# A mixed order of tiles in layer 1 of a graph attention kernel

## The chip, the cores and the metric

The kernel runs on one core of a Trainium2 chip. The core has five engines with a queue of instructions each: TensorE (PE in the profile; its weight loads are shown apart as PEld), VectorE (DVE), ScalarE (ACT), GpSimd (POOL) and SyncE (SP), and 16 DMA engines that all queues share. Instructions of one engine run in order; engines wait for each other by semaphores. The metric is the device time of one execution in microseconds (us).

## The reference

Two layers of graph attention (GAT) over 10,000 nodes with 768 numbers each and 170,000 edges (80,000 random pairs in both directions, and a self-loop for each node), sorted by destination. Layer 1 has 4 heads of 256, layer 2 one head of 768. Cut to what matters:

```python
def gat_conv(x, edge_index, W, a_src, a_dst, bias, heads, out_ch, concat):
    ei = _add_self_loops(edge_index, n)
    src, dst = (ei[0], ei[1])
    xl = (x @ W).reshape(n, heads, out_ch)
    alpha_src = einsum('nhc,hc->nh', xl, a_src)
    alpha_dst = einsum('nhc,hc->nh', xl, a_dst)
    e = leaky_relu(alpha_src[src] + alpha_dst[dst], 0.2)
    m = segment_max(e, dst)
    e = exp(e - m[dst])
    alpha = e / (segment_sum(e, dst)[dst] + 1e-16)
    out = segment_sum(xl[src] * alpha[:, :, None], dst)
    return out + bias
...
h = gat_conv(x, edge_index, W1, a_src1, a_dst1, b1, HEADS, HID, True)
h1 = relu(layer_norm(h, g1, be1)) + (x @ Wr1 + br1)
h = gat_conv(h1, edge_index, W2, a_src2, a_dst2, b2, 1, OUT_DIM, False)
h = layer_norm(h, g2, be2) + (h1 @ Wr2 + br2)
return _layernorm(x + h)
```

## The kernel before

**Preparation** (up to about 760 us). A table is computed, `table1`: for each node a row of 1,033 numbers (4,132 bytes) with its 1,024 projected features, its attention terms and its rank. Beside it the nodes are counted and ranked by how many edges end in them, most edges first. The 10,000 nodes make 79 tiles of 128 nodes in rank order, so the nodes of a tile have about the same number of edges. A tile t gets a fixed number of slots, `SLOTS[t]`, from a bound on the number of edges at that rank: 41 for tile 0, 27 for tile 1, then 26, 25, 24 and so on down to 7 for tile 78, 1,371 in all. A slot is one row for each of the 128 nodes: the row of one neighbour. The word "rows" of the change means these slots. `slots` (128 x 1,371 integers) lists the neighbours to gather, tile after tile in the order of `TURNS`; `FIRST[t]` is the first column of a tile.

**Layer 1** (`ordered_layer1`) goes through the tiles in the order of `TURNS`; a position in that order is what its loop counts as `t`. Before, `TURNS` takes every second tile from the smallest to the largest and the others back again: 7, 10, 11, 12, 12, 13, ... 22, 22, 23, 24, 26, 41, 27, 25, 24, 23, 22, 22, ... 12, 12, 11, 11, 9 rows. For each slot POOL issues one indirect DMA (`gather`, L472) that brings 128 rows of `table1` into one of the 31 places of `ring` (`RING1`); `ring.fetch`, called once a slot, issues the gather for a place as soon as the row that lay there has been used, so up to 31 rows are on their way or waiting. For positions 1 and 2 a limit of their own, `upto`, holds fetches back.

What is done for a tile at position t:

- `weights_of` makes the attention weights: POOL adds the terms (`summed_logits`, L939 to L944), DVE and ACT take the leaky maximum, the exponent and the sum (`exponents`, L956). It is begun during the last rows of the tile before (`soon`, three or four rows before its end).
- Tiles of 22 rows or more (`PARTED`) do this in groups: two groups, the last of 8 rows, or three groups of 17, 12 and 12 for the 41 (`cuts_of`). A later group is rescaled into the sum of the earlier ones (L1204), and its first one to three rows are summed by PE and copied by ACT (L1014).
- The first rows of a tile, none up to five (`on_pe`: 0 for 11 rows, 1 for 12 and 13, 2 for 14 and 15, 3 for 16 and 17, 4 for 18 and 19, 5 from 20 on), are scaled by ACT in place (L562, four scalings a row, one for each head) and summed by PE in PSUM with an identity matrix (L933). The other rows are added by DVE: either scaled by ACT first and added in one instruction (L569), or scaled and added by DVE (L573).
- Meanwhile the tile before is finished: its statistics (L584, two instructions a tile, on DVE), its normalisation and residual (L598, L600, L1078) make `h`; PE transposes `h` (L896), computes the residual product of the present tile `x @ Wr1` (L179) and multiplies `h` by W2 (L1150, `to_layer2`); ACT copies the outcome (L1042), and SP stores it as a part of `table2` (L1044) and stores `hT` (L1142) for layer 2.
- In a tile without groups, PE also transposes the x of the next tile ahead of time (`turn`); behind a tile with groups this is done at the start of the next tile.

**Layer 2** (`ordered_layer2`) goes over the tiles again in an order of its own, `turns`, which is made by sorting the positions of layer 1 by size and taking large and small ones by turns; it gathers rows of `table2` by rank and writes the result.

The lines that set the order before the change:

```python
    TURNS = list(range(NT - 1, -1, -2))
    TURNS += sorted(set(range(NT)) - set(TURNS))
    FIRST, TOTAL = [0] * NT, 0
    for t in TURNS:
        FIRST[t], TOTAL = TOTAL, TOTAL + SLOTS[t]
```

Of the kernel before, what the change touches and what calls it, by code (L numbers as in the profile page):

```python
# [57 lines left out]
WHOLE = 4  # L58
PARTED = 22
FEW = 11  # L60


def chunk_counts(n_edges):
# [23 lines left out]
def gnn_kernel(ctx, tc, x, x_cols, src, dst, src_col, dst_col, W1, a_src1, a_dst1, b1, g1, be1, Wr1, br1,  # L87
# [9 lines left out]
    NT = -(-N // P)  # L97
# [3 lines left out]
    CAPS = slot_counts(N, n_edges)  # L101
    SLOTS = CAPS

    TURNS = list(range(NT - 1, -1, -2))
    TURNS += sorted(set(range(NT)) - set(TURNS))
    FIRST, TOTAL = [0] * NT, 0
    for t in TURNS:
        FIRST[t], TOTAL = TOTAL, TOTAL + SLOTS[t]
# [446 lines left out]
    def doubled(e, t):  # L555
        nc.vector.tensor_scalar(e[:, 0], e[:, 0], loops[:, TURNS[t]:TURNS[t] + 1], None, op0=OP.mult)

# [276 lines left out]

    SLOTS, FIRST = [SLOTS[t] for t in TURNS], [FIRST[t] for t in TURNS]
    SLOTS1, FIRST1 = SLOTS, FIRST
    turns = sorted(range(NT), key=lambda t: SLOTS[t] + 2 * (t >= NT - 2))
    first, left, final = turns[:3], turns[3:-3] + turns[-1:], turns[-3:-1]
    mean, mixed = sum(SLOTS[t] for t in left) / len(left), []
    while left:  # L840
        few = sum(SLOTS[t] for t in mixed) <= mean * len(mixed)
# [27 lines left out]
    def nodes(t):  # L869
        return order[:, TURNS[t]:TURNS[t] + 1]  # L870

    def ordered_layer1(mem):
        nc.scalar.add_instruction(mybir.InstLoadActFuncSet(name=nc.get_next_instruction_name(), act_func_set_id=6, engine=nc.scalar.engine))
        with tc.tile_pool(name="b1", bufs=1) as pool, tc.tile_pool(name="small1", bufs=2) as small, \
# [42 lines left out]
            def on_pe(t):  # L917


                return min(max(SLOTS[t] // 2 - 5, int(SLOTS[t] > FEW)), ON_PE1)  # L920

# [25 lines left out]
            def exponents(e, top=None):  # L947

                n = e.shape[1]
                leaky(e, e)  # L950
                new = small.tile([P, H1], F32, name="new")
                nc.vector.reduce_max(new, e.rearrange("p k h -> p h k"), axis=AX.X)
                if top is not None:
                    nc.vector.tensor_max(new, new, top)
                nc.vector.tensor_tensor(e, e, new[:, None, :].to_broadcast([P, n, H1]), op=OP.subtract)
                nc.scalar.activation(e, e, AF.Exp)  # L956
                return new

            def weights_of(t):
# [11 lines left out]
                top = exponents(e)  # L971
                nc.scalar.activation(e[:, 0], e[:, 0], AF.Copy, scale=loops[:, TURNS[t]:TURNS[t] + 1])
                yield {0: (e, None)}
# [722 lines left out]
```

## Time and profile before

| | |
|---|---|
| median of 3 runs | 5296.87 us (5289.57 to 5301.86) |
| the profiled execution, its own time | 5288.65 us |
| span of the profiled execution | 5286.9 us |
| mean granted clock of TensorE | 0.946 |
| HBM read and written | 1426.26 MB and 177.29 MB |
| DMA of the software queue (gathers) | 1283.72 MB |

The page gives, for the slowest core of one execution, the busy time of each engine and its share of the span. Below stand 40 equal slices of the span (132 us each), where a digit is the busy share in tenths; the row PEclk is the clock that TensorE was granted, in tenths of full speed. Groups of instructions are named by line, engine, operation and the tiles written and read (`out<-in`), with the number of instructions, the busy time and the mean duration. Idle time of an engine is put down to what released it (`<-`). A view of stretches gives the busy times, the granted clock and the DMA figures for any part of the span.

### The profile page before, as it was taken

How to read it: one execution, taken by the hardware profiler on the slowest of the kernel's cores; microseconds unless marked ns; L12 is line 12 of the kernel's file. 1: busy time of each engine (PE TensorE's matmuls, PEld its weight loads, DVE VectorE, ACT ScalarE, POOL GpSimd, SP SyncE). 2: the span in 40 equal slices, each digit the busy share in tenths (PEclk: the TensorE clock that was granted, in tenths of full speed). 3: DMA queues.
4: the chain of work that ended last, by engine and by line, in shares of the span. 5: the costliest groups of instructions: out<-in, count | busy, mean ns of one | idle time of the engine just before them, and what ended most of it. 6: DMA issues, size and time to landing. Idle time of an engine off the chain costs nothing. (4 is left out here: it accounts for less than half of the span.)

```text
span 5286.9 us, 58012 instructions
## 1 busy us (share of the span) xinstructions
PE 4759.0 (90%) x14100; PEld 2659.8 (50%) x14100; DVE 4343.1 (82%) x7341; ACT 2986.1 (56%) x8450; POOL 3429.6 (65%) x3722
## 2 busy tenths in 40 slices
PE   9999988999999978899999997888888888888886
PEld 4444444555544434444555554555555555555554
DVE  7887877999989988889999985877777776777776
ACT  5744446888889988898888762232222222222222
POOL 6877756666677766677666626666666666666664
PEclk9999999999999998999999998898899898888898
DMA  4423459999999989999999959988898888888885
GB/s 153 131 98 127 113 176 337 350 358 369 381 379 393 376 298 339 342 367 377 382 367 360 351 213 313 325 320 316 314 321 315 311 313 310 312 305 300 306 312 191
DMA packets 433439, 1588.37 MB, mean 300 GB/s; under 512 B 77207, under 2 KB 82135, under 8 KB 433094
## 3 DMA queue, kind: packets, MB, share of 16 engines
q0 software_dynamic: 321040, 1283.72, 67.7%
q1 hardware_dynamic: 99490, 269.38, 14.1%
q10 hardware_dynamic: 12564, 31.47, 1.9%
q8 instruction: 119, 1.95, 0.2%
q14 instruction: 226, 1.85, 0.1%
HBM read 1426.26 MB, written 177.29 MB: 303 GB/s over the span
## 5 line engine op out<-in xcount | busy, mean ns | idle before, releaser
L472 POOL DMA_INDIRECT ring<-table,slots x2663 | 2633.5, 989 | 1496.1 <-issue 564.8
L562 ACT ACTIVATE ring<-ring,e 128x256 f32<-128x256 f32 x4208 | 1714.4, 502 | 62.9 <-DVE e L978 36.6
L573 DVE SCALAR_TENSOR_TENSOR acc<-ring,e,acc 128x256 f32<-128x256 f32 (+1 forms) x2540 | 1581.3, 623 | 106.4 <-PE acc L933 21.5
L569 DVE TENSOR_TENSOR acc<-acc,ring 128x1024 f32<-128x1024 f32 x782 | 962.9, 1231 | 77.9 <-ACT ring L562 17.6
L1342 PE MATMUL big<-wr,w 128*128 128x512 f32 (+1 forms) x2464 | 870.0, 499 | 129.2 <-issue 127.7
L1288 PE MATMUL big<-ring,diagonals 128*128 128x256 f32 x2742 | 723.6, 419 | 187.7 <-issue 172.6
L1150 PE MATMUL half<-w,hT 128*128 128x512 f32 (+1 forms) x2528 | 842.5, 486 | 3.6 <-issue 3.5
L179 PE MATMUL big<-wr,xT 128*128 128x512 f32 x1896 | 836.6, 598 | 0.3 <-ACT xT L897 0.3
L1288 PEld LDWEIGHTS big<-ring,diagonals 128*128 128x128 f32 x2742 | 581.5, 213 | 324.5 <-issue 226.1
L1287 ACT ACTIVATE diagonals<-ident,e 128x128 f32<-128x128 f32 x1371 | 420.6, 388 | 533.6 <-PE big L1288 227.0
L1342 PEld LDWEIGHTS big<-wr,w 128*128 128x128 f32 x2464 | 478.1, 195 | 484.7 <-issue 455.2
L1150 PEld LDWEIGHTS half<-w,hT 128*128 128x128 f32 x2528 | 472.6, 189 | 346.4 <-issue 310.6
L179 PEld LDWEIGHTS big<-wr,xT 128*128 128x128 f32 x1896 | 358.5, 193 | 422.3 <-issue 421.6
L933 PE MATMUL acc<-ring,ident 128*128 128x512 f32 x1080 | 495.9, 609 | 58.5 <-ACT ring L562 51.4
L588 ACT ACTIVATE sd<-mv,eps 128x1 f32<-128x1 f32 x237 | 69.3, 292 | 688.5 <-issue 362.0
L933 PEld LDWEIGHTS acc<-ring,ident 128*128 128x128 f32 x1080 | 205.8, 194 | 307.4 <-issue 188.5
L694 ACT ACTIVATE scr<-scr 128x256 f32<-128x256 f32 x624 | 250.5, 403 | 160.5 <-DVE scr L687 152.5
L634 PE MATMUL one<-wr,mixed 128*128 128x512 f32 x702 | 307.6, 592 | 0.0
L699 POOL TENSOR_TENSOR row<-row,none 128x1024 f32<-128x1024 f32 x69 | 168.1, 2437 | 115.2 <-DVE scr L687 45.0
L634 PE MATMUL one<-w,xT 128*128 128x512 f32 x492 | 226.8, 597 | 7.9 <-DMA w<-in_W_dram 5.6
L584 DVE BATCH_NORM_STATS2 st<-big 128x6 f32<-128x256 f32 x79 | 33.4, 422 | 234.4 <-remote 125.6
L634 PEld LDWEIGHTS one<-wr,mixed 128*128 128x128 f32 x702 | 133.4, 190 | 167.9 <-issue 166.9
(239 smaller groups left out, 4328.1 us busy)
## 6 DMA issues: line engine op xcount, KB each, us to landing
ring<-table,slots POOLq DMA_INDIRECT x2663
h_d<-hT SPq DMA_DIRECT2D x79, 512.0 KB
table<-row SPq DMA_DIRECT2D x78, 516.0 KB
w<-h_d SPq DMA_DIRECT2D x77, 512.0 KB
table<-row SPq DMA_DIRECT2D x79, 385.0 KB
ring<-table SPq DMA_DIRECT2D x79, 385.0 KB
x_d<-xt SPq DMA_DIRECT2D x77, 384.0 KB
w<-x_d SPq DMA_DIRECT2D x77, 384.0 KB
```

The lines of the kernel that those rows point to most:

```text
L179: nc.tensor.matmul(p[:, c:e], aT[:, j, :], w[:, j, c:e], start=(j == 0), stop=(j == k - 1))
L472: nc.gpsimd.indirect_dma_start(out=to, out_offset=None, in_=table, in_offset=bass.IndirectOffsetOnAxis(ap=index, axis=0), **more)
L562: nc.scalar.activation(row[:, s], row[:, s], AF.Copy, scale=e[:, h:h + 1])
L569: nc.vector.tensor_add(acc[:, :c], acc[:, :c], row[:, :c])
L573: nc.vector.scalar_tensor_tensor(acc[:, s], row[:, s], e[:, h:h + 1], (acc if first is None else first)[:, s], op0=OP.mult, op1=OP.add)
L634: nc.tensor.matmul(p, aT[:, j, :], w[:, j, :], start=(start and j == 0), stop=(j == k - 1), skip_group_check=True)
L694: nc.scalar.activation(m[:, s], m[:, s], AF.Copy, accum_out=row[:, C1 + i * H1 + h:C1 + i * H1 + h + 1])
L933: nc.tensor.matmul(acc[:, c:c + BANK], ident, ring.slot(q + k)[:, c:c + BANK], start=(k == 0), stop=(k == m - 1))
L1150: nc.tensor.matmul(q, hT[:, j, :], w2[:, j, c:c + q.shape[1]], start=(j == 0), stop=(j == K1 - 1))
L1287: nc.scalar.activation(diagonals[:, (k - lo) % G, :], ident, AF.Copy, scale=e[:, k - lo, :])
L1288: nc.tensor.matmul(to, diagonals[:, (k - lo) % G, :], ring.slot(at + k)[:, ON_PE2:C2], start=False, stop=(k == n - 1), skip_group_check=True)
L1342: nc.tensor.matmul(r[:, c:d], hT[:, j, :], wr2[:, j, c:d], start=False, stop=(j == K1 - 1 and d < C2), skip_group_check=True)
```

## The change

Only `TURNS` is made in another way. Seven tiles are set aside for the two ends (`ENDS`): the smallest four of every second one (7, 10, 11, 12 rows) begin and 11, 11, 9 end. The 72 others are picked one by one: from the largest while the mean of those picked is not above the mean of all tiles, otherwise from the smallest. The list is then turned round, so that the largest tile comes last in it.

```diff
+ENDS = 7
...
-    TURNS = list(range(NT - 1, -1, -2))
-    TURNS += sorted(set(range(NT)) - set(TURNS))
+    TURNS, few, left = [], [NT - 1 - t for t in range(min(ENDS, NT))], list(range(NT - len(range(min(ENDS, NT)))))
+    while left:
+        more = sum(SLOTS[t] for t in TURNS) <= sum(SLOTS) * len(TURNS) / NT
+        TURNS.append(left.pop(0 if more else -1))
+    TURNS = few[::2] + TURNS[::-1] + few[1::2][::-1]
```

The rows of the tiles in order, after:

```
7 10 11 12 22 21 21 21 21 20 20 20 20 20 20 19 19 19 19 19 19 18 18 18 18 18 18 18 18 17 17 17 17 17 17 17 16
22 16 16 16 22 16 16 16 16 22 15 15 23 15 15 23 15 15 15 24 14 14 24 14 14 25 14 14 13 26 13 13 27 13 13 12 12 12 41 11 11 9
```

## The prediction, made before the change was run

> **What bounds the kernel now.** I read the page's totals and slices first.
>
> ```profile
> span 5286.9 us, 58012 instructions
> PE 4759.0 (90%) x14100; PEld 2659.8 (50%) x14100; DVE 4343.1 (82%) x7341; ACT 2986.1 (56%) x8450; POOL 3429.6 (65%) x3722
> PE   9999988999999978899999997888888888888886
> PEclk9999999999999998999999998898899898888898
> DMA  4423459999999989999999959988898888888885
> ```
>
> PE is 90% busy over the whole span, but the change touches layer 1 alone, so the question is what paces that stage. In the slices it runs from about 760 to 3150 us, with PE and DMA near full except for a dip around 1850 to 2250, where the 22- to 41-row tiles stand together. Where a tile ends I read from the first of its two statistics on DVE (L584, two a tile); I cut the trace at those. First four longer stretches of layer 1, then its middle tile by tile (columns: stretch and length, busy time of PE, weight loads, DVE, ACT, POOL with their counts, granted clock, DMA share, GB/s).
>
> ```profile
> L584 DVE BATCH_NORM_STATS2 st<-acc x38: 679/689/699, 1699.2 to 2402.1; 128x6 f32<-128x512 f32 x38
> ...
> 906.10:1248.90 342.80, 339.07 (x1037) 179.02 (x1036) 315.91 (x457) 280.15 (x714) 220.39 (x274) 1.00 0.97 354
> 1480.50:1732.63 252.13, 245.52 (x714) 124.23 (x713) 224.41 (x313) 232.73 (x593) 180.46 (x216) 1.00 1.01 387
> 1877.80:2157.40 279.60, 231.31 (x607) 112.08 (x606) 235.36 (x404) 230.51 (x580) 186.47 (x245) 0.91 0.89 319
> 2157.40:2236.20 78.80, 68.68 (x183) 33.59 (x183) 65.54 (x114) 63.51 (x162) 51.96 (x67) 0.93 0.94 337
> ...
> 1699.19:1732.63 33.44, 31.40 (x91) 15.54 (x90) 28.48 (x38) 30.95 (x79) 22.81 (x28) 1.00 1.01 387
> 1732.63:1767.90 35.27, 33.75 (x93) 16.51 (x92) 32.51 (x56) 32.56 (x84) 25.78 (x36) 1.00 0.99 364
> 1767.90:1802.50 34.60, 33.22 (x95) 16.39 (x95) 32.48 (x56) 31.96 (x82) 25.45 (x35) 1.00 1.01 385
> 1802.50:1839.20 36.70, 33.45 (x95) 16.42 (x95) 34.50 (x61) 32.21 (x82) 26.80 (x37) 1.00 0.99 377
> 1839.20:1877.80 38.60, 36.01 (x101) 17.53 (x101) 34.57 (x61) 34.64 (x88) 27.97 (x35) 1.00 0.97 366
> 1877.80:1922.50 44.70, 37.87 (x101) 18.27 (x100) 35.89 (x62) 36.14 (x92) 26.81 (x37) 0.96 0.89 322
> 1922.50:1990.30 67.80, 42.31 (x110) 19.84 (x109) 56.77 (x97) 55.62 (x141) 48.11 (x64) 0.84 0.73 252
> 1990.30:2037.30 47.00, 43.49 (x110) 20.69 (x109) 37.90 (x66) 37.98 (x96) 30.95 (x38) 0.91 0.92 331
> 2037.30:2079.40 42.10, 36.35 (x96) 17.92 (x95) 35.77 (x62) 34.67 (x88) 27.29 (x38) 0.92 0.94 335
> 2079.40:2119.50 40.10, 37.17 (x102) 18.54 (x101) 34.51 (x61) 34.70 (x88) 27.88 (x35) 0.96 0.97 353
> 2119.50:2157.40 37.90, 34.13 (x93) 16.82 (x93) 34.51 (x60) 31.40 (x80) 25.43 (x37) 0.95 0.98 365
> 2157.40:2195.40 38.00, 33.47 (x90) 16.31 (x90) 32.44 (x57) 32.10 (x82) 25.91 (x33) 0.93 0.94 342
> 2195.40:2236.20 40.80, 35.22 (x94) 17.29 (x93) 33.10 (x58) 31.40 (x81) 26.05 (x35) 0.92 0.93 332
> 2236.20:2271.40 35.20, 33.83 (x100) 17.15 (x99) 29.23 (x41) 30.75 (x80) 23.75 (x29) 0.97 0.96 342
> 2271.40:2303.70 32.30, 31.08 (x91) 15.60 (x90) 29.11 (x41) 30.60 (x80) 24.43 (x30) 1.00 1.00 379
> 2303.70:2339.70 36.00, 32.04 (x91) 15.91 (x90) 27.99 (x40) 29.91 (x78) 22.01 (x26) 0.96 1.00 372
> ```
>
> The first long stretch holds 13 tiles of 13 to 16 rows: 26.4 us each, of which PE is busy 26.1 and DVE 24.3. A small tile is paced by PE, and DVE has 2.1 us to spare in it. The tiles from 1732.63 on have 22, 22, 23, 24, 26, 41, 27, 25, 24, 23, 22, 22 rows; a 21 stands before them, and 21, 21, 20 after. From 21 to 22 rows DVE's own work jumps from 28.48 to 32.51 us, while PE's busy time holds sums that go at ACT's pace (timeline below); I take the big tiles as paced by DVE and by what DVE waits for. The same sizes cost different times on the two sides of the 41: going up, two 22s took 35.27 and 34.60 at clock 1.00; coming down, 38.00 and 40.80 at 0.93 and 0.92. DVE's own work hardly differs (32.5 against 32.4 and 33.1), so the difference is waiting. DVE's waits in the pair going up, then in the pair coming down, and last the only wait of the logits for gathered rows in layer 1:
>
> ```profile
> DVE h L600 <- ACT sd L588: 0.5, 1, 0.5
> DVE acc L573 <- issue: 0.3, 1, 0.3
> ...
> DVE acc L1204 <- ACT ring L1014: 3.6, 1, 3.6
> DVE acc L1204 <- issue: 3.5, 1, 3.5
> DVE acc L573 <- PE acc L933: 2.0, 1, 2.0
> ...
> POOL e L941 <- DMA ring<-table,slots: 4.7, 2, 2.5
> ```
>
> Coming down, DVE waits 9.1 us for PE's sums, which are late because PE begins the tile at a lower clock; so DVE computes the next tile's weights late, PE stands still before them, and the clock falls again. The timeline shows both starts of a tile:
>
> ```profile
> 1762.79 6.49 ACT L562 ACTIVATE ring<-ring,e 128x256 f32<-128x256 f32 x16
> 1763.75 9.11 PE L933 MATMUL acc<-ring,ident 128*128 128x512 f32 x20 [1.52 <-ACT ring L562]
> 1774.49 1.09 PE L896 MATMUL half<-ident,h 128*128 128x128 f32 x8 [0.97 <-DVE acc L573]
> ...
> 2191.23 11.80 PE L933 MATMUL acc<-ring,ident 128*128 128x512 f32 x20 [3.07 <-ACT ring L562]
> 2232.72 7.67 PE L933 MATMUL acc<-ring,ident 128*128 128x512 f32 x11 [5.13 <-ACT ring L562]
> ```
>
> After an idle 1.52 us the twenty matmuls of the first sums took 9.11 us; after 3.07 us they took 11.80. I take this for a loop that the row of big tiles keeps going from the 26 to the first 20 behind them. DMA, though 0.97 to 1.01 busy, is not waited for: 4.7 us in 2400.
>
> **The change part by part.** It adds and removes no instruction: the same 79 tiles, 1371 gathers and 12 tiles cut in groups (22 rows or more). It moves tiles. Positions 0 to 3 keep 7, 10, 11, 12 rows and the last three keep 11, 11, 9. Between them stand 22, 21 four times, 20 six times, then 19s to 16s going down, and from position 37 one big tile to every two to four small ones: 22, 22, 22, 23, 23, 24, 24, 25, 26, 27 and at position 75 the 41. Preparation writes the same lists to other columns (nothing there depends on the column), so I cost it at nothing. Layer 2 sorts its own order by size: it comes out with the same sequence of sizes, and its gathers read table rows numbered by rank, which do not move: nothing. The allowance for fetches in tile 2 rises from 57 to 67, but the ring of 31 stops it at 59: two gathers some microseconds earlier, nothing.
>
> *The big tiles.* Each now comes after a small, PE-paced tile at full clock, as the first 22 did. I price them by the rising side. 22s: 4 at 34.9 (mean of 35.27 and 34.60) is 139.7 against 35.3 + 34.6 + 38.0 + 40.8 = 148.7: -9.0. 23s: 2 at 36.7 against 74.6: -1.2. 24s: 2 at 38.6 against 78.7: -1.5. For 25, 26 and 27 there is no undisturbed row; I take DVE's busy time plus what the 24 going up had over it (38.60 - 34.57 = 4.0): 39.8 + 39.9 + 41.9 = 121.6 against 133.8: -12.2. The 41 stays at 67.8; DVE's 56.77 sets it wherever it stands. The 21 and the 20 in the tail of the loop took 35.2 and 36.0; undisturbed, a 21 takes 32.9 (33.44 and 32.30), and a 20 takes 31.5 (252.13 over the eight tiles of 19 to 21 rows at 1480.50): -6.8. Together -30.7.
>
> *The exits.* Before, a big tile had a tile without groups behind it once; now twelve times. There PE has nothing left over: it adds the first rows of the next tile and then waits for that tile's transposes of h. In 22 after 22 five rows go to PE and the wait is 0.97 us. A row costs ACT four scalings, 6.49 / 16 x 4 = 1.6 us, and PE follows ACT. With 3 rows (size 16), 2 (14, 15) or 1 (13), PE has 2, 3 or 4 rows fewer: it idles about 4.2, 5.8 or 7.5 us, 5.5 in the middle. Small tiles behind it win some back, because DVE needs only 24.3 of their 26.4 us: two of them give 4.2. Net +1.3 an exit. Bounds: -2.1, if the small tile simply runs at DVE's pace, to +8.2, which is what the one exit in the trace cost (40.80 + 35.20 against 34.9 + 32.9) with the clock already low. I take +1.3 since that exit stood within the loop: 12 x 1.3 = +15.6.
>
> *Start and end.* The start now meets a 22 at position 4 where a 12 stood. Its first group of 14 rows and the rest need 10 rows more by the end of that tile than before; the ring issues them 8 or more rows ahead, as between two 21s now. Nothing, with 0 to 5 us as bounds (twice the longest DMA wait, 2.5). After the 41, the last three tiles find their 31 rows in the ring; they run PE-paced as now.
>
> The sum: -30.7 + 15.6 = -15. The profiled execution took 5288.65 us (span 5286.9), so 5273.5; the median of the runs, 5296.87, lies 8.2 above it: **5282 us**, 0.3% faster. Its own range: exits free, 5266, to exits that eat the gain, 5297.
>
> A rule speaks against it. The Trainium skill ("TensorE: Matmul & The Clock Gate", the section on HAM oscillation) has it that one idle window of about 3.4 us halves PE's clock until a busy window restores it. The trace agrees in kind: clock 1.00 behind gaps of 1.5 us, 0.92 with gaps of 3.07 and 5.13. By its figures each exit would lose an estimated 1.7 us more, 20 us for twelve, and the sum would be +5.
>
> **The rivals.**
>
> *The clock falls at every exit* (slower). The gaps of 4 to 7 us worked out above are longer than the 3.07 that preceded the slow sums. Price from the two rows: 11.80 - 9.11 = 2.7 us an exit, on a tile that PE paces, so on the path: 12 x 2.7 = 32, and -15 + 32 = +17: 5314. It decides from 2.1 us an exit on ((15 + 10.6) / 12, to be slower by over 0.2%). At the 8.2 of the measured exit it would be -30.7 + 98 = +68. Against it: small tiles leave DVE 2.1 us each, and PE's sums there are short.
>
> *DMA is the bound and gets evened out* (faster by more). For: shares near 1.00 at 387 GB/s in the stretch before the dip, 319 and 337 in the dip. Filling the dip to about 380 wins (380 - 319) x 279.6 + (380 - 337) x 78.8 MB/1000 = 20.4 MB, 54 us: 5243. Against: only 4.7 us of waits for gathers, and the 41's low rate comes with DVE at 56.77 of 67.80. Big tiles at little over DVE's busy time beside small ones with DVE to spare would give about the same time.
>
> *Nothing that can be measured changes*: a tile's time belongs to its size, the falling side is slow for a reason of its own, and the exits balance: 5297. Against: the two pairs of 22s.
>
> **How the numbers follow.** The forecast 0.45, the clock rival 0.30, evening-out 0.13, nothing 0.12. The range goes from the evening-out case, 5243, a little below, to beyond the clock rival, 5330: 5240 to 5330; the far exits (5365) are left out. About 0.2% (10.6 us) is what a measurement can tell from no change. Faster by more: four fifths of the forecast and the evening-out case, 0.49; within it: the rest of the forecast and the third rival, 0.20; slower: 0.31.
>
> **What would show it.** Right: 22s at about 35 us with clock 1.00, the 27 near 42, small tiles behind big ones at 25 to 28 us, and the 20s and 21s between 30 and 34. The loop is refuted if isolated 22s still take 38 or more. The clock rival shows as a granted share under 0.95 in most tiles behind a big one, and as sums there at about 1.3 times their time. DMA as the bound would show as logits waiting for gathers, now 4.7 us. Layer 2, from about 3200 to the end at 5286.9, should keep its length; a difference there, or preparation that ends later than 760 us, would make the prediction wrong whatever layer 1 does, and so would a start that waits for rows in positions 4 to 8.

## The result, and the profile after

The changed kernel takes 5340.44 us (median of 6 runs, 5337.40 to 5349.07), the kernel before on the same chip 5287.96 us (6 runs, 5284.93 to 5301.86): a ratio of 1.0099 [1.0086, 1.0112]. The change makes the kernel 1% slower, 52 us. The forecast was 5282, on the other side. The page of the kernel after, its totals and its slices:

```profile
span 5335.6 us, 57998 instructions
...
PE 4759.9 (89%) x14100; PEld 2662.2 (50%) x14100; DVE 4343.9 (81%) x7341; ACT 2983.2 (56%) x8450; POOL 3428.5 (64%) x3710
...
PE   9999988999999999989998977887888888888886
...
PEclk9999999999999999999999988988989898898888
DMA  4323459999999999999999958988899988898885
```

The same matmuls and the same busy time stand in a span that is 48.7 us longer. The dip in the middle of layer 1 is gone, as meant: PE and DMA are now full to the end of it. Yet it ends later. The view of stretches of the kernel before, layer 1 and layer 2 (from the first statistics of the last tile of layer 1):

```profile
762.00:3153.47 2391.47, 2252.74 (x6565) 1152.57 (x6564) 2120.37 (x3170) 1978.67 (x5028) 1570.81 (x1954) 0.98 0.95 353
...
3153.47:5286.90 2133.43, 1761.12 (x5824) 1184.35 (x5822) 1595.57 (x3186) 596.34 (x1863) 1323.55 (x1371) 0.89 0.87 304
```

The same view of the kernel after: the two layers, then single tiles (a 22, the 16 behind it; a 24, the 14 behind it; a 27, the 13 behind it; the 41). Columns as in the prediction.

```profile
762.00:3204.17 2442.17, 2266.59 (x6566) 1162.58 (x6565) 2120.70 (x3170) 1975.61 (x5028) 1563.11 (x1942) 0.97 0.94 345
...
3204.17:5335.60 2131.43, 1748.41 (x5824) 1176.74 (x5822) 1595.90 (x3186) 596.62 (x1863) 1329.41 (x1371) 0.89 0.87 305
...
1901.54:1941.58 40.04, 37.24 (x102) 18.73 (x101) 32.97 (x58) 34.78 (x90) 26.61 (x36) 0.96 0.96 348
1941.58:1968.42 26.84, 25.32 (x80) 13.22 (x79) 25.21 (x37) 22.77 (x60) 18.90 (x22) 1.00 1.00 380
...
2483.47:2526.85 43.38, 37.65 (x104) 19.18 (x103) 34.98 (x63) 35.19 (x90) 27.12 (x37) 0.94 0.94 337
2526.85:2551.53 24.68, 23.03 (x67) 11.05 (x66) 23.20 (x33) 20.33 (x53) 16.33 (x20) 0.96 0.98 354
...
2891.09:2942.76 51.67, 44.39 (x120) 22.19 (x118) 38.18 (x67) 38.57 (x97) 30.08 (x40) 0.92 0.87 304
2942.76:2967.72 24.96, 21.11 (x54) 10.59 (x54) 23.11 (x33) 19.57 (x50) 14.79 (x19) 0.82 0.90 312
3065.47:3135.52 70.05, 46.78 (x131) 23.69 (x129) 57.03 (x100) 55.43 (x140) 45.20 (x58) 0.86 0.69 239
```

All of it is in layer 1: 2442.17 against 2391.47, +50.7; layer 2 is 2.0 shorter. Cutting every tile in this way gives the classes: the twelve big tiles went from 503.6 to 550.3 us (+46.6), those of 18 to 21 rows from 745.7 to 751.9, all smaller ones from 1142.2 to 1140.0. So the big tiles hold the loss: a 22 takes 40 and not 35, a 24 takes 43.4 and not 38.6. The tiles behind them, where the prediction put its cost, lose next to nothing: 26.84, 24.68, 24.96.

What does DVE wait for? First the kernel before, then the kernel after, in layer 1 (us in total, times, longest):

```profile
DVE acc L573 <- PE acc L933: 21.5, 23, 2.4
...
DVE h L600 <- ACT sd L589: 13.6, 6, 4.1
```

```profile
DVE h L604 <- ACT sd L593: 66.1, 21, 5.8
DVE acc L577 <- PE acc L937: 40.0, 31, 2.4
```

(The code after stands four lines lower: L604 is L600 of before, L577 is L573, L937 is L933.) Two waits grew: for `sd`, the reciprocal deviation that ACT computes between its scalings, and for PE's sums. At the twelve entries into a big tile the wait for `sd` alone is 46.8 us (beyond the 0.1 us that this instruction waits at any entry before), as much as the whole loss. That it is not the cause is what the experiments show.

The timeline at one entry shows why both come late. Before, a 21 and then the first 22 (the statistics at 1732.63 are the border):

```profile
1725.02 3.65 PE L1150 MATMUL half<-w,hT 128*128 128x258 f32 x16
...
1729.08 6.50 ACT L562 ACTIVATE ring<-ring,e 128x256 f32<-128x256 f32 x16
1730.05 8.86 PE L933 MATMUL acc<-ring,ident 128*128 128x512 f32 x20 [1.38 <-ACT ring L562]
1732.63 1.29 DVE L584 BATCH_NORM_STATS2 st<-acc 128x6 f32<-128x512 f32 x2
...
1738.80 1.06 PE L896 MATMUL half<-ident,h 128*128 128x128 f32 x8
```

After, a 16 and then a 22 (border at 1901.54):

```profile
1899.15 0.82 PE L900 MATMUL acc<-ident,xt 128*128 128x128 f32 x6
...
1899.81 3.65 PE L1154 MATMUL half<-w,hT 128*128 128x258 f32 x16
1900.01 0.86 ACT L901 COPY xT<-acc 128x512 f32<-128x512 f32 x2 [3.69 <-PE acc L900]
1900.75 6.49 ACT L566 ACTIVATE ring<-ring,e 128x256 f32<-128x256 f32 x16
1901.54 1.29 DVE L588 BATCH_NORM_STATS2 st<-acc 128x6 f32<-128x512 f32 x2
1903.29 8.75 PE L937 MATMUL acc<-ring,ident 128*128 128x512 f32 x20
...
1907.70 1.28 DVE L604 SCALAR_TENSOR_TENSOR h<-h,sd,norm 128x1024 f32<-128x1024 f32 x1 [3.23 <-ACT sd L593]
```

Before, PE ends `to_layer2` at 1728.67, 4.0 us ahead of the border, even waits 1.38 us for ACT, and its five sums end 6.3 us behind the border. After, PE ends `to_layer2` at 1903.46, 1.9 us behind the border; it transposed the x of the 22 so late that ACT stood 3.69 us for it and began the scalings 0.8 us before the border instead of 3.6. The sums end at +10.5, DVE's `h` waits behind the scalings, and DVE, which paces a big tile, does everything after that later. Over the twelve big tiles the sums ended 4.9 to 7.8 us behind the border before (66.2 us added up), and 9.1 to 13.1 after (135.3 us).

### The profile page after: what moved, and what is told of

The parts are those of the page before. It is cut to its first block, busy times and chain, and to the rows that moved or that the text cites. A ratio compares the mean times of both kernels' runs of the same rounds, so it can differ in the third digit from the quotient of the medians.

```text
span 5335.6 us, 57998 instructions
## 1 busy us (share of the span) xinstructions
PE 4759.9 (89%) x14100; PEld 2662.2 (50%) x14100; DVE 4343.9 (81%) x7341; ACT 2983.2 (56%) x8450; POOL 3428.5 (64%) x3710
## 5 line engine op out<-in xcount | busy, mean ns | idle before, releaser
L577 DVE SCALAR_TENSOR_TENSOR acc<-ring,e,acc 128x256 f32<-128x256 f32 (+1 forms) x2540 | 1581.2, 623 | 123.2 <-PE acc L937 40.0
L573 DVE TENSOR_TENSOR acc<-acc,ring 128x1024 f32<-128x1024 f32 x782 | 962.9, 1231 | 66.5 <-ACT ring L566 9.1
L1292 PE MATMUL big<-ring,diagonals 128*128 128x256 f32 x2742 | 710.4, 413 | 203.1 <-issue 171.6
L937 PE MATMUL acc<-ring,ident 128*128 128x512 f32 x1080 | 510.3, 624 | 76.4 <-ACT ring L566 75.2
L937 PEld LDWEIGHTS acc<-ring,ident 128*128 128x128 f32 x1080 | 212.8, 200 | 331.5 <-issue 188.9
```

The source lines that it names most:

```text
L573: nc.vector.tensor_add(acc[:, :c], acc[:, :c], row[:, :c])
L577: nc.vector.scalar_tensor_tensor(acc[:, s], row[:, s], e[:, h:h + 1], (acc if first is None else first)[:, s], op0=OP.mult, op1=OP.add)
L937: nc.tensor.matmul(acc[:, c:c + BANK], ident, ring.slot(q + k)[:, c:c + BANK], start=(k == 0), stop=(k == m - 1))
L1292: nc.tensor.matmul(to, diagonals[:, (k - lo) % G, :], ring.slot(at + k)[:, ON_PE2:C2], start=False, stop=(k == n - 1), skip_group_check=True)
```

## The experiments

Four theories, named in the expectations by what they blame. **A**: the entry, as ACT has it; `sd` stands behind the copies of x and sixteen scalings. **B**: the exit, the prediction's own cost. **C**: the entry, as PE has it; PE is nearly always busy in a small tile and comes into the next tile with work left over, so that its five sums start late. **D**: layer 1 simply has too much PE work, wherever it lies. Each run stands against the kernel before on its own chip; the first four ran on one chip (before: 5328.55 us), the next four on another (4940.84), the last four on a third (4941.20). The changed kernel itself has a profile from the chip of the result and one from the third (run 9); its big tiles took 550.3 and 545.7 us there. Where runs 1 to 8 are set beside it tile by tile, that is across chips.

**1. x is not transposed ahead for a big tile**, so that neither ACT's copies nor PE's transposes of it stand ahead of the entry:

```diff
-                turned, turn = [], live and 0 < t < NT - 1 and len(cuts) == 2
+                turned, turn = [], live and 0 < t < NT - 1 and len(cuts) == 2 and len(cuts_of(t + 1)) == 2
```

> The changed order, but a small tile ahead of a tile with groups no longer transposes that tile's x ahead of time; it is done at the big tile's start, as between two big tiles before. Theory A (entry): at the end of a small, PE-paced tile ACT stands still 2.2 to 5.4 us for PE's late transposes of x, only then scales the big tile's first rows (16 scalings, 6.5 us), and only then gives DVE the deviation of the finished tile; DVE waits 1.7 to 5.7 us for it at 12 entries, 46.7 us in all, which is the whole excess of the big tiles (46.6 us). Without the copies ahead the wait falls below 1 us; the transposes cost about 1 us at the big tile's start: 5340 - 40 + 12 = about 5310 (5298 to 5320). Theory B (exit): the excess comes from the end of the big tile, where PE idles 4 to 7 us and its clock falls; nothing of that is touched: 5335 to 5345.

5366.68 us, 1.0076 [1.0057, 1.0095]. The wait for `sd` at the twelve entries went from 46.8 us to 0.0. The big tiles went from 550.3 to 545.0 only, and PE's sums at the entries still end 8.5 to 12.4 us behind the border. DVE's waits of this run in layer 1:

```profile
DVE acc L577 <- PE acc L937: 76.9, 25, 6.8
DVE h L604 <- ACT sd L593: 24.6, 9, 5.8
```

The wait for PE's sums has grown by 36.9 us in place of the other's 41.5. DVE meets the same lateness one instruction later: `sd` was the first sign of it, not its cause.

**2. The copies of x one row later** in every tile without groups:

```diff
-                    events.append((soon + (on_pe(t + 1) < 4), moved))
+                    events.append((soon + 1, moved))
```

> The changed order, with ACT's copies of the next tile's x put behind the scalings of that tile's first three rows wherever it has four or more rows on PE (for fewer it is so already). Theory A: ACT scales three rows while it would have stood still, so the deviation comes 3 to 5 us earlier at most entries: about 5305 (5295 to 5320), and the wait for the deviation falls from 46.7 us at the 12 entries to under 15. Theory B (exit): no change, 5335 to 5345.

5404.55 us, 1.0151 [1.0131, 1.0171]: slower. The wait for `sd` at the entries fell to 2.1 us, the big tiles stayed at 550.2, and the tiles of 18 to 21 rows rose from 751.9 to 789.8. A 21 of this run:

```profile
965.02:1003.00 37.98, 32.73 (x90) 16.35 (x90) 29.08 (x41) 30.74 (x80) 23.47 (x30) 0.96 0.94 334
```

In the changed kernel a 21 took 33.1 to 34.0. By the code, the x is transposed into the PSUM that the next tile's sums use, so ACT's copies have to leave it before PE can start; PE waited 4.28 us for them ahead of this 21, and 35.7 us in layer 1. The edit acts ahead of every tile with four or five rows on PE, the big ones among them. There the wait for `sd` is nearly gone, and the big tiles gained nothing; A falls.

**3. The deviation before the first scalings**, by starting the normalisation ahead of the first step of the weights:

```diff
-                next(later, None)
                 if last and not early:
                     norm = started()
+                next(later, None)
```

> The changed order, with the finished tile's statistics and deviation asked for ahead of the scaling of the fourth row, instead of behind it, in every tile. Theory A: four scalings, 1.6 us, no longer stand before the deviation at the 12 entries: 5340 - 12 x 1.6 = about 5320, and the waits go from 46.7 to about 28. Theory B (exit): 5335 to 5345.

5363.30 us, 1.0067 [1.0048, 1.0086]. The waits for `sd` at the entries fell from 46.8 to 27.7 us, as meant; the big tiles took 549.7. It is the third cut of this wait, and the big tiles keep their time.

**4. Every exit leads to a 20 or 21.** Ten of the 20s and 21s each go behind a big tile (it is the only change of order; the entries stay):

```diff
+    for t in range(10):
+        TURNS.remove(21 - t)
+        TURNS.insert(TURNS.index(10 - t) + 1, 21 - t)
```

> The changed order, but the ten tiles of 20 and 21 rows stand behind ten of the big tiles (small, big, 20 or 21, small), instead of together near the start. A big tile is still entered from a small one; what follows it has five rows for PE, as between big tiles before, so PE's gap and its clock at the exit are those of the old order. Theory A (entry): the entries cost what they cost, 5332 to 5348. Theory B (exit): ten exits at 3 to 4 us each are saved, 5300 to 5315.

5374.27 us, 1.0088 [1.0070, 1.0105]. The big tiles took 555.3 us, a 22 behind a 16 still 40.12. With five rows for PE to go on with at ten of the exits, nothing is won: B falls, as the times of the tiles behind big ones had already said.

**5. Less PE work in the small tile ahead of a big one.** The residual product of those small tiles is summed over half of the 768 numbers of x (three of six slices of 128); the rest of their residual is left out.

```diff
-                        r = product(xT, wr1, C1, ps_r)
+                        short = SLOTS[t] < 18 and t + 1 < NT and SLOTS[t + 1] >= PARTED
+                        r = product(xT, wr1[:, :K0 // 2] if short else wr1, C1, ps_r)
```

> The changed order with half of the residual product x @ Wr1 left out (three of six slices of 128) in the 12 small tiles right ahead of a big one, about 5 us of PE's work each. Theory C (PE's backlog): a small tile leaves PE 0.5 to 4.5 us of its product with W2 behind the tile's end on DVE, where a 21 before a 22 left it 4.0 us ahead; the big tile's five sums so end 9 to 13 us into the tile instead of 5 to 6, and DVE, which paces the tile, starts that much later. Freed of 5 us the sums end at about 5 to 7 and the big tiles go back to the prices of the rising side: 12 x 4 to 5, ratio to the kernel before about 1.000 (0.998 to 1.003). Theory B (exit): the exits stay, and only PE-paced small tiles get shorter, by at most the 1.5 us by which DVE is shorter there: 12 x 1.5 = 18, ratio 1.006 to 1.007.

4952.69 us, 1.0021 [1.0011, 1.0031]: most of the loss is gone. Its timeline at the same entry, a 16 and then a 22 (border at 1861.39), and then its stretches, that 22, a 24 and the 25:

```profile
1855.81 2.34 PE L1155 MATMUL half<-w,hT 128*128 128x258 f32 x10
...
1856.80 6.49 ACT L566 ACTIVATE ring<-ring,e 128x256 f32<-128x256 f32 x16
...
1857.99 8.75 PE L937 MATMUL acc<-ring,ident 128*128 128x512 f32 x20
...
1861.39 1.29 DVE L588 BATCH_NORM_STATS2 st<-acc 128x6 f32<-128x512 f32 x2
```

```profile
1861.39:1897.07 35.68, 32.29 (x89) 15.78 (x88) 32.98 (x59) 30.98 (x80) 27.29 (x36) 1.00 1.00 383
...
2422.88:2461.31 38.43, 32.68 (x88) 16.01 (x87) 34.88 (x62) 31.36 (x80) 27.98 (x37) 0.97 1.00 383
...
2601.47:2641.50 40.03, 34.38 (x92) 16.75 (x91) 36.19 (x63) 33.13 (x85) 28.94 (x38) 0.94 0.98 377
```

PE is done 3.2 us ahead of the border, the sums end at +5.3, and the tile takes 35.68 us where it took 40.04: DVE waits 0.5 us in it, where it waited 5.0. The twelve big tiles take 495.4. The small tiles ahead of them, which do less, don't get shorter (313.1 us for the twelve, 314.6 in run 9): what PE saves there is won in the next tile. C stands, unless any saving of PE's would do the same; run 10 asks that.

**6. Less PE work by fewer rows on PE** in the small tile ahead of a big one (all its rows go to DVE):

```diff
+                if SLOTS[t] < 18 and t + 1 < NT and SLOTS[t + 1] >= PARTED:
+                    return 0
```

> The changed order; the small tile right ahead of a big one gives none of its rows to PE (it gave 1 to 3), DVE adds them all. Theory C: PE's backlog at the big tile falls by 1.2 to 1.6 us a row, 1.5 to 5 us, and the sums end that much earlier; DVE pays about 1.5 us a row in the small tile, of which it has 2 us to spare: net 1 to 2 us an entry, ratio 1.005 to 1.008. Theory B (exit): the small tiles get longer by DVE's rows and nothing is won: 1.010 or more.

5017.38 us, 1.0149 [1.0132, 1.0166], not what C was expected to give, and by the number what B said (1.010 or more). PE came to the border at most 2.2 us earlier than in run 9 (once 0.2 later), and a 16 without rows on PE took 30.22 us, 28.38 of them DVE's work, where one took 26.3. The big tiles gained 12.7 us against run 9, with sums that end 12.5 us earlier, and the twelve small ones ahead of them lost 26.2. So C was right on the big tiles; what the run adds is that DVE had no room for these rows.

**7. Big tiles in pairs.** Five of them are moved directly behind another, so that only seven are entered from a small tile:

```diff
+    for t in range(9, 0, -2):
+        TURNS.remove(t)
+        TURNS.insert(TURNS.index(t + 1) + 1, t)
```

> The changed order with ten of the big tiles put together in pairs (22 22, 22 23, 23 24, 24 25, 26 27), between twice as many small ones. Theory C: the second of a pair is entered from a big tile, which leaves PE ahead, so it costs the price of the rising side, 4 to 8 us less: 27 us in all, ratio 1.0045 (1.003 to 1.0065). If a big tile's price were its own, whatever stands before it: 1.009 to 1.010.

4975.02 us, 1.0066 [1.0049, 1.0083]. The stretches of one pair, a 23 behind a 15 and then a 24, and of the other 24, which stands behind a 14:

```profile
2314.64:2356.28 41.64, 37.90 (x103) 19.07 (x102) 34.57 (x61) 35.55 (x91) 25.84 (x34) 0.96 0.94 334
2356.28:2394.81 38.53, 34.44 (x97) 17.25 (x96) 34.98 (x62) 31.73 (x81) 28.12 (x37) 0.98 0.99 370
...
2526.52:2571.34 44.82, 41.58 (x114) 21.15 (x113) 34.63 (x60) 39.11 (x100) 27.59 (x35) 0.96 0.92 323
```

A 24 costs 44.82 us behind a small tile and 38.53 behind a big one, less than the 23 ahead of it. The sums of the first of a pair end 10.3 to 12.3 us behind the border, those of the second 4.9 to 6.4. Of twelve entries five are gone, and of the loss about half (34 us over its kernel before, against 67 in run 9 on the third chip).

**8. All twelve big tiles in one row**, in the midst of the mixed order, entered once from a 16:

```diff
+    hump = [10, 8, 6, 4, 2, 0, 1, 3, 5, 7, 9, 11]
+    place = TURNS.index(10) - 1
+    TURNS = [t for t in TURNS if t not in hump]
+    TURNS = TURNS[:place] + hump + TURNS[place:]
```

> The changed order without the mixing: the big tiles stand together again (22 22 23 24 26 41 27 25 24 23 22 22) behind a 16, and the small ones go down behind them; the 21s and 20s stay near the start. Theory C: one entry from a small tile is left, about 5 us; ratio 1.001 (0.999 to 1.003). If the loss came from the other parts of the change (21s right after the start, smaller tiles only at the end): 1.006 to 1.010.

4952.05 us, 1.0023 [1.0014, 1.0033]. The stretches of its first two 22s:

```profile
1828.93:1868.43 39.50, 37.89 (x107) 19.23 (x106) 32.49 (x56) 35.41 (x91) 22.81 (x31) 1.00 0.94 338
1868.43:1903.58 35.15, 33.21 (x95) 16.42 (x95) 32.55 (x57) 32.08 (x82) 26.71 (x37) 1.00 1.00 382
```

One entry, one loss of 4.4 us, at clock 1.00. The big tiles take 488.9 in all. All other tiles keep the mixed order's sequence; only the entries are gone, and most of the loss with them.

**9. The changed kernel, and 11. the kernel before, both on the third chip**, as yardsticks for run 10:

> The changed kernel itself, on the chip of the next three, as their yardstick. All theories: ratio 1.008 to 1.011 to the kernel before.

> The kernel before, with a profile on this chip, to compare stage by stage. If the falling side of the big tiles is slow by a loop that the 41 sets off, the 25, 24, 23, 22, 22 behind the 27 take 42, 40, 38, 38, 41 us again; if that was one execution's accident, they take 38 to 39, 38, 37, 35, 35 as in the run with the big tiles behind a 16.

5008.04 us against 4941.20, 1.0136 [1.0120, 1.0151]; expected was what the first chip gave, 1.008 to 1.011, so the change costs more here. Layer 1 ends 57.5 us later. The big tiles take 545.7 us in run 9, nearly what they took on the first chip, but 482.4 in run 11, and not 503.6. The stretches of run 11 behind its 27: 25, 24, 23, 22, 22 rows, of which four are shown.

```profile
2021.87:2060.25 38.38, 34.12 (x97) 16.78 (x97) 35.76 (x61) 34.32 (x88) 27.32 (x39) 1.00 0.98 367
2060.25:2098.51 38.26, 35.76 (x101) 17.51 (x101) 34.51 (x60) 34.37 (x88) 27.90 (x35) 1.00 1.00 374
...
2135.16:2169.71 34.55, 33.24 (x95) 16.44 (x95) 32.44 (x57) 32.00 (x82) 25.89 (x33) 1.00 1.01 379
2169.71:2205.39 35.68, 32.56 (x93) 16.03 (x93) 33.12 (x59) 31.32 (x81) 25.93 (x34) 1.00 1.00 370
```

The falling side, on which the prediction built its gain (42.1, 40.1, 37.9, 38.0, 40.8), isn't slow here at all: 38.4, 38.3, 36.6, 34.6, 35.7 at clock 1.00. It was a matter of the first chip, or of its execution, and not of the order. With this yardstick the entries explain the loss in size, too. The sums end 131.3 us behind their borders in run 9, added over the twelve big tiles, and 64.9 us in run 11: 66.4 later, and the big tiles are 63.3 longer.

**10. The same PE work taken from other tiles**: the half product of run 5, but in the eleven small tiles directly behind a big one, not the twelve ahead of one (the residual is left out there in the same way):

```diff
-                        r = product(xT, wr1, C1, ps_r)
+                        short = SLOTS[t] < 18 and t > 3 and SLOTS[t - 1] >= PARTED
+                        r = product(xT, wr1[:, :K0 // 2] if short else wr1, C1, ps_r)
```

> The counterpart of the run with half of the residual product left out ahead of the big tiles: the same half is left out in the 11 small tiles right behind a big one. Theory C (PE's backlog at the big tile's entry): the small tile behind is paced by DVE, and one or two small tiles build the backlog anew, so the sums at the entries still end 9 to 12 us into the big tile: ratio 1.007 to 1.010, within 0.002 of the changed kernel. Theory D (the stage simply has too much work for PE around the big tiles, wherever it lies): 11 x 4 to 5 us less as before, ratio 1.000 to 1.003.

5000.19 us, 1.0123 [1.0107, 1.0138], 7.9 us below run 9 (1.7 of them in layer 1) and so 59 above the kernel before, where run 5 was 12 above its own. Its timeline at the entry from a 16 to a 22 (border at 1862.77):

```profile
1861.03 3.65 PE L1155 MATMUL half<-w,hT 128*128 128x258 f32 x16
...
1862.77 1.29 DVE L588 BATCH_NORM_STATS2 st<-acc 128x6 f32<-128x512 f32 x2
...
1864.52 8.75 PE L937 MATMUL acc<-ring,ident 128*128 128x512 f32 x20
...
1868.92 1.28 DVE L604 SCALAR_TENSOR_TENSOR h<-h,sd,norm 128x1024 f32<-128x1024 f32 x1 [3.23 <-ACT sd L593]
```

PE ends `to_layer2` 1.9 us behind the border, as in the changed kernel, and the big tiles take 545.5 us. Where the saving goes can be seen behind a relieved 14, at the border at 2513.51:

```profile
2515.24 5.40 PE L937 MATMUL acc<-ring,ident 128*128 128x512 f32 x8 [3.36 <-ACT xT L901]
```

PE is done early, then stands 3.36 us for ACT's copies, and starts the next sums 1.7 us behind the border. It isn't how much PE does in layer 1 but whether it is done when a big tile starts. D falls; C is shown from both sides.

The runs on the second and third chip can be put side by side. In each, the ends of PE's first sums behind their borders are added up over the twelve big tiles:

| run | sums end late by, in all | the twelve big tiles take |
|---|---|---|
| 12, the 41 moved (below) | 64.7 us | 485.6 us |
| 11, before | 64.9 us | 482.4 us |
| 8, one row | 71.5 us | 488.9 us |
| 5, half product ahead | 78.2 us | 495.4 us |
| 7, pairs | 104.8 us | 518.1 us |
| 6, no rows on PE | 118.8 us | 533.0 us |
| 10, half product behind | 131.2 us | 545.5 us |
| 9, the change | 131.3 us | 545.7 us |

Whatever was changed, a microsecond by which PE's sums end later is about a microsecond more in the big tiles.

**12. The order of before with the 41 behind the row of big tiles**, in case the 41 sets off the slow falling side:

```diff
+    TURNS.remove(0)
+    TURNS.insert(TURNS.index(11) + 1, 0)
```

> The order of before with one tile moved: the 41 comes last of the big ones, between the second 22 of the falling side and the 21s, instead of between 26 and 27. It is still entered from a big tile. If the 41 sets off the slow falling side (its end leaves PE idle for 20 us at half clock): 27, 25, 24, 23, 22, 22 go to about 42, 39.8, 38.6, 36.7, 35, 35 from 47.0, 42.1, 40.1, 37.9, 38.0, 40.8, and the 21 behind the 41 takes 2 to 4 us more: 15 us less, ratio 0.997 (0.995 to 0.999), faster than both kernels. If the falling side is slow of itself: 0.999 to 1.001.

4943.07 us, 1.0005 [0.9996, 1.0014]: nothing won, as on this chip there is no slow falling side to win (big tiles 485.6 us against 482.4). Run 11 says something on the 41 by itself: PE idles 17.35 us at its end there, and the granted clock is 0.50 from 1960 to 1970 us, yet the tiles from the 25 on aren't slow. So the 41 alone doesn't set a slow falling side off. No version that was run beats the kernel before.

## Why the prediction was wrong

- **What bounds layer 1** was read rightly in part: DMA isn't the bound, big tiles are DVE-paced, and DVE's wait for PE's sums was the sign to follow. That PE, busy 26.1 of 26.4 us, paces a small tile doesn't hold as it stands: with 5 us less of PE's work (run 5) those tiles kept their length. PE's lateness falls due in the next tile. Preparation and layer 2 kept their time (2131.43 against 2133.43). At the start, the 22 at position 4 took 43.3 us, 3.3 more than the dearest of those behind a 16, but its sums also end latest of all (13.1 us behind the border); in run 9, where they end at +9.5, it took 39.25. So this is PE's lateness again rather than a wait for rows, though it was not tried by itself.
- **The step that failed**: "Each now comes after a small, PE-paced tile at full clock, as the first 22 did. I price them by the rising side." The first 22 came after a 21, and a 21 leaves PE 4.0 us ahead of the border; the other tiles of the rising side came after big ones, which leave it 4.6 to 7.2 us ahead. Behind a tile of 12 to 16 rows PE is late: its `to_layer2` runs out 0.5 to 4.5 us behind the border, and 8.8 us of sums come after it. The prediction had both halves of this (PE is full in small tiles; the big tile waits for PE's sums) and didn't put them together. Instead of -23.9 the big tiles gave +46.6. The trace of the kernel before could have told, at the border between two small tiles. Here it is a 14 and a 14, with the border at 2938.17:

```profile
2938.07 3.65 PE L1150 MATMUL half<-w,hT 128*128 128x258 f32 x16
```

  PE ends 3.6 us behind the border, where the row at 1725.02 has it 4.0 us ahead. Over that trace the lateness goes by the size of the tile that ends: on the average PE is 3.7 us ahead behind a 21, 0.1 ahead behind an 18, 0.9 late behind a 16, 3.1 behind a 14 and 4.4 behind a 12. The residual product takes PE 10.47 us in an 18 as in a 14, and the last part of `to_layer2` 3.65 in both, so in a shorter tile they run further past its end. The rising prices themselves were good where PE isn't late: run 5 has 35.0 to 35.7, 37.2 and 37.6, 38.4 and 39.0, 40.0 for 22 to 25 rows, against 34.9, 36.7, 38.6, 39.8. For 26 and 27 they were too low: 44.5 and 46.0 against 39.9 and 41.9.
- **The falling side as a loop** that the row of big tiles keeps going: read from one execution. It is absent on the third chip with the same order (run 11), so most of the gain of 30.7 rested on something that the order doesn't make. What makes it on the first chip is open; run 12 could not tell, having run where it doesn't occur. The 9.1 us of waits that the prediction laid to PE's sums are 2.0 us for the sums, 3.6 for ACT's copies and 3.5 for which the profile names no releaser. The prediction's own sign against the loop came, too: the 22s now stand alone, and they take 39.6 to 43.3 us. The tail's -6.8 didn't come either (18 to 21 rows: +6.2).
- **The exits**: +1.3 each was priced, about -0.3 was found (26.8 and 28.1 against a mean of 27.4 for a 16 before, 24.6 to 24.7 against 25.7 for a 14). The mechanism is there. In the kernel after, at the exit from a 24 to a 14:

```profile
2524.62 5.72 PE L937 MATMUL acc<-ring,ident 128*128 128x512 f32 x8 [5.73 <-ACT ring L566]
```

  PE idled 5.73 us (estimate: 5.8), and eight matmuls then took 5.72 us, more than the 0.44 each of the 8.75 for twenty. But DVE doesn't wait for PE in that tile: the 14 took 24.68. The case of the lower bound, a small tile that runs at DVE's pace, is what happened, though with -0.3 on the average and not the -2.1 that it was given; the reason that the prediction gave against the upper bound ("that exit stood within the loop") should have led there.
- **The rival of the falling clock** gave the sign and a third of the size (+17 of 52 us), and its mechanism is not what happened. The clock does fall behind such gaps (0.82 in the 13 behind the 27). But DVE doesn't wait for PE's first sums there, and run 8 has the entry's loss at clock 1.00, and so have two 22s of run 9 (40.04 and 39.62 us). The Trainium skill ("TensorE: Matmul & The Clock Gate", the section on HAM oscillation) has the fall of the clock behind such gaps in kind. The 20 us that were estimated from that section for twelve exits don't appear.
- The largest omission: the prediction priced what happens behind a big tile in three ways, and what happens ahead of it in none. (By its four cases the chances come to 0.49, 0.21 and 0.30, and not to 0.49, 0.20 and 0.31; nothing hangs on that.)

## What to carry to other kernels

Where stages with different limiting engines alternate, look at every border for which engine arrives late, and price a moved stage behind the neighbours it will have, not behind those that it had. When a wait seems to hold the whole loss, take it away before believing it: here 46.8 us of waiting were removed twice and the big tiles stayed as long, once with the next wait on the same engine in its place, because the lateness began on PE, one tile earlier. An asymmetry found in one execution is worth a look at a second chip before a forecast is built on it.

## What the runs showed of the hardware

The chips differ by more than any version here: the same kernel before takes 5328.55, 4940.84 and 4941.20 us on the three chips of the experiments, and 5287.96 in the runs of the result. Most of it is in layer 2. The same 1600 us of it, in the kernel before on the first chip, and in run 11 on the third:

```profile
3300.00:4900.00 1600.00, 1341.62 (x4434) 901.74 (x4434) 1228.02 (x2458) 455.52 (x1431) 1023.18 (x1060) 0.89 0.89 313
```

```profile
3300.00:4900.00 1600.00, 1468.51 (x5256) 1024.36 (x5255) 1437.73 (x2875) 532.16 (x1697) 1205.99 (x1246) 0.96 0.98 366
```

Seventeen per cent more bytes a second, 18% more instructions of POOL, most of them gathers (1246 against 1060), and a granted clock of 0.96 against 0.89. Which of these is the cause isn't shown. In layer 1 the same two executions differ by 44 us of 2391. The ratio of one change, too, came out differently on two chips: 1.0099 and 1.0136, intervals that don't meet.
